# Graph layer 0 of a four-layer GNN kernel: sums of the second half's rows moved, block sums left to accumulating transfers

## The chip, the core and the metric

One core of a Trainium2 chip runs the whole program. The metric is the device time of one execution in microseconds (us), the median of several executions; lower is better.[...] PE is the matrix engine (TensorE), DVE the vector engine, ACT the scalar engine, POOL the GpSimd engine, SP the engine that issues most transfers.

## What is computed

```
# adj: 2708 x 2708, x: 2708 x 512
h = relu(layernorm(x));  d = (rowsum(adj) + 1) ** -0.5
x = x + relu(diag(d) (adj + I) diag(d) h @ W0)                  # layer 0
h = relu(layernorm(x));  x = x + norm(adj) h @ W1.T + b1          # layer 1
h = relu(layernorm(x));  x = x + relu(norm(adj + I) h @ W2)       # layer 2
h = relu(layernorm(x));  x = x + gated attention(h, adj)          # layer 3
```

Everything is float32. Only layer 0 is touched by the change.

## The kernel before

**Tiling.** The 2708 nodes are four quarters of 677. A quarter is five tiles of 128 rows and a tail; the tails of all quarters fill tiles 20 and 21. `h` holds the normalised features of all 22 tiles; "first half" means tiles 0 to 9 (quarters 0 and 1), "second half" tiles 10 to 21. The transposed adjacency lies in DRAM as blocks `yb[j, i, u]` of 128 x 1695 numbers (847.5 KB): quarter j of the sum, quarter i of the outputs, and u (0 or 1) one half of that quarter's 678 columns. 339 columns is the width of every large matmul.

**Two levels of fast matrix products.** `adj @ h` is done by seven outer products (a Strassen-Winograd form over halves) instead of eight: `OUTER` (line 376 after, the same table before) names for product p the feature operand (XA, XB, XC, XD are the two halves of `h` by the two halves of the features, overwritten as the work goes on) and the block operand: y11, y21, y22 as they lie in DRAM or the sums T1 = y12 + y11, T3 = y22 + y12, T2 = T3 + y11, T4 = T2 + y21, each with a multiple of the unit matrix. Every outer product is done for u = 0 and u = 1 by `multiply`, which is again seven products ("pieces") of five 128 x 339 matmuls: pieces 1, 6, 2, 7, 5, 4, 3 in program order. Before it, `inner_x` makes four small feature sums (128 x 640) and `inner_y` makes four block sums t1, t2, t3, t4 (128 x 1695 each) on DVE. Piece 6 reads t2, piece 7 reads t3, piece 5 reads t1, piece 4 reads t4. Behind the pieces DVE adds the results (`u2`, `u3`, `give`) out of PSUM into `agg`.

**Layer 0 has its own order**, `first_aggregate`. Row sums of `adj` must be known before `h` can be scaled, so the first half's degrees are summed on PE (`column_sums`: matmuls with a 32-column operand `first`) while the blocks arrive, then product 1 runs for u = 0, 1, then product 7 (u = 0, 1), and during product 7 the second half's degrees are summed (`other_degrees`): three blocks' worth per u out of T3's inner sums. Behind the second of these come twelve one-column matmuls that turn row sums into columns (line 346), roots on ACT and DVE (`rsqrt`, `rstd_of`), and the normalising activations of the second half (line 221, 128 x 512 each). Product 6 needs XA := -XD - XA (line 682), so it needs those. Then products 6, 2, 4 for u = 1 and again for u = 0, the tail rows (`tails`, quarters 0 and 1), product 5 (u = 0, 1), `tails` (2, 3), and the epilogue (line 754 and on).

**Block sums before.** T3 is made from two plain loads each (y22 and y12) and a DVE add (`third_sums`, line 644); T2 by DVE (line 651); both are also written to DRAM (`keep_o`, line 398) for later layers. T4 by DVE (line 723). T1 is made by a plain load of y12 and an accumulating transfer of y11 onto it (`first_sums`, line 697: `dma_start(..., accum_op=ALU.add)` on POOL's queue), then the unit matrix (line 410) is added by DVE.

**What sets the order.** A tile scheduler places each engine's instructions by readiness and program order; `tc.issue_after(i)` keeps the instructions in its scope behind instruction i in that placing. SP issues plain loads[...]; POOL issues stores and accumulating transfers. Waits come from buffers: `free` is a list of 847.5 KB buffers, and `more`, `early`, `spare` are buffers cut out of areas that layer 0 does not yet need (`ends`, `agg`, and the second half of `h`).

Of the kernel before, what the change touches and what calls it, by code (L numbers as in the profile page):

```python
# [8 lines left out]
FP = mybir.dt.float32  # L9
AF = mybir.ActivationFunctionType  # L10
ALU = mybir.AluOpType
# [26 lines left out]
def gnn_kernel(  # L38
# [172 lines left out]

    def shift_of(mv, scale, n):

        b = small_cols("sh", n)
        nc.vector.scalar_tensor_tensor(
            b[:, :n], mv[:, :n, 0], -1.0, scale[:, :n], ALU.mult, ALU.mult
        )
        return b

    def normalized(t, src, scale, shift):  # L220
        nc.scalar.activation(h[:, t, :], src, AF.Relu, bias=shift, scale=scale)

# [19 lines left out]
    def first_stats(ts):  # L242
        for t in ts:
            stats(h[:, t, :], mv0[:, t, :])


# [66 lines left out]

    def other_degrees(u, ys):

        if u == 0:
            parts[1, 1] = upool.tile([P, W], FP, tag="s", name="row")
        for b, blocks in ((0, (ys[1], ys[2])), (1, (ys[7],))):
            ps = ps_out.tile([P, W], FP, tag="out", name="dg_ps")
            tl = tail_place(b, u)  # L320
            column_sums(ps, [tl[:, 0], tl[:, 1]], blocks, parts[b, u])
        if u < U - 1:
            return
        columns = {}
        for b in range(2):
            columns.update(quarter_columns(2 + b, [parts[b, v] for v in range(U)]))
        columns.update((t, tail_columns(t)) for t in (NF, NF + 1))
        first_h(columns, NF - half)
# [10 lines left out]
    def first_h(columns, looped):  # L339
# [18 lines left out]
        nc.vector.tensor_mul(rstd[:, :n], rstd[:, :n], dinv[:, span])  # L358
        sh = shift_of(mv, rstd, n)
        for s, t in enumerate(ts):  # L360
            normalized(t, h[:, t, :], rstd[:, s : s + 1], sh[:, s : s + 1])

# [59 lines left out]


    at_u2, at_u3, at_end, at_t4 = [], [], [], []

# [16 lines left out]
    def inner_y(blks, u, loops, t3=None):  # L442
        o11, o12, o21, o22 = blks
        if loops:
            add_loops(o11, u, loops)
            add_loops(o22, u, loops)
        t1, t2, t4 = (tpool.tile([P, KT, W], FP, tag="t", name=f"t{k}") for k in (1, 2, 4))
        t3 = o12 if t3 is None else t3
        nc.vector.tensor_add(t1, o12, o11)  # L449
        nc.vector.tensor_add(t2, o22, t1)  # L450
        at_t4.append(nc.vector.tensor_add(t4, o21, t2).ins)  # L451
        nc.vector.tensor_add(t3, o22, o12)
        return {1: o11, 2: o21, 3: o22, 4: t4, 5: t1, 6: t2, 7: t3}
# [12 lines left out]

    def multiply(xs_, ys, u, dests):

# [14 lines left out]
        def give(a, b, ps, part, op):  # L483
# [5 lines left out]
            for fh, ih, how in dests:  # L489
# [3 lines left out]
                elif how == "added":  # L493
                    nc.vector.tensor_add(d, d, ps)
                elif how == "less":
                    nc.vector.tensor_sub(d, ps, d)
                else:
                    nc.scalar.copy(d, ps)
# [3 lines left out]
        v = upool.tile([P, W], FP, tag="v", name="v")  # L502
        nc.scalar.copy(v, pa)  # L503
        pb = bank("pb")
# [10 lines left out]
        product(pd, 5, True)  # L515
        give(1, 1, pd, u3, ALU.subtract)
        product(pc, 4, False)
        give(1, 0, pc, u2, ALU.add)
# [32 lines left out]
    def tails(self_loops, qs, loaded=None):  # L551

        for q in qs:
            blk, both = loaded[q] if loaded else tail_rows(self_loops, q)
            for u in range(U):
# [8 lines left out]
                for c in range(NC):  # L564
                    d = agg[:, c // 2, q // 2, c % 2, q % 2, u * W : (u + 1) * W]
                    nc.vector.tensor_add(d, d, ps[c])
            free.append(blk)
# [38 lines left out]
    def first_aggregate(epilogue):  # L606
# [9 lines left out]
        pieces = [(q, u) for q in range(2) for u in range(U)]  # L616
        places = spare + early
        for q, u in pieces:
# [11 lines left out]


        t3 = {0: [free.pop(0), free.pop(0), take(early), take(early)], 1: blks[0]}
        temps = spare + [take(early)]
        p1, p7 = (0, 0, "as it is"), (1, 1, "as it is")
        for u in range(U):
            for b in range(2):
                load_rows(*(tail_place(b, u)[:, s] for s in range(2)), yt[:, :, 2 + b, u])
        xs_ = inner_x(XA)
        multiply(xs_, ys, 0, [p1])
        ys = inner_y(blks[1], 1, 0, own_t3)  # L640

        def third_sums(u):
            for (a, b), blk, y in zip(QUAD, t3[u], temps):
                nc.vector.tensor_add(blk, blk, y)
                if a == b:
                    add_loops(blk, u, OUTER[7][2])
                keep_o(blk, "t3", a, b, u)

        def second_sums(u):
            for (a, b), t2, y in zip(QUAD, blks[u], t3[u]):  # L650
                nc.vector.tensor_add(t2, t2, y)
                keep_o(t2, "t2", a, b, u)

        for (a, b), blk, y in zip(QUAD, t3[0], temps):
            load_plain("y22", a, b, 0, blk)
            load_plain("y12", a, b, 0, y)
        with tc.issue_after(at_u2[-1]):
            third_sums(0)
        for (a, b), y in zip(QUAD, temps):
            load_plain("y12", a, b, 1, y)  # L660
        multiply(xs_, ys, 1, [p1])
        second_sums(0)
        by_halves(nc.vector.tensor_sub, XA, XA, XB)
        xs_ = inner_x(XA)
        ys = inner_y(t3[0], 0, 0, own_t3)
        last_sum = at_t4[-1]
        other_degrees(0, ys)
        for (a, b), blk in zip(QUAD, t3[1]):
            load_plain("y22", a, b, 1, blk)
        multiply(xs_, ys, 0, [p7])  # L670
        with tc.issue_after(last_sum):
            third_sums(1)
        first_x(range(half, NT))
        ys = inner_y(t3[1], 1, 0, own_t3)
        with tc.issue_after(at_u3[-1]):
            second_sums(1)
        with tc.issue_after(at_end[-1]):
            first_stats(range(half, NT))
        other_degrees(1, ys)
        multiply(xs_, ys, 1, [p7])  # L680
        first_part_of_both()
        by_halves(minus_sum, XA, XD, XA)
        free += t3[0][:2] + t3[1]

        def among(places):
# [4 lines left out]
            return free.pop(0)  # L690


        def first_sums(u, places):
            t1 = [among(places) for _ in QUAD]
            for (a, b), blk in zip(QUAD, t1):
                load_plain("y12", a, b, u, blk)
                nc.gpsimd.dma_start(blk, yb[a, b, u], accum_op=ALU.add)
            with tc.issue_after(at_u3[-1]):
                for (a, b), blk in zip(QUAD, t1):
                    if a == b:  # L700
                        add_loops(blk, u, OUTER[5][2])
                    keep_o(blk, "t1", a, b, u)
            return t1

        for u in reversed(range(U)):
            if u == 1:
                t2 = blks[1]
            else:
                t2 = [among(in_obuf) for _ in QUAD]
                for (a, b), blk in zip(QUAD, t2):  # L710
                    nc.sync.dma_start(blk, osum["t2", a, b, u])
            xs_ = inner_x(XA)
            multiply(xs_, inner_y(t2, u, 0, own_t3), u, [(0, 1, "added")])
            if u == 1:
                other_roots()
                nc.vector.tensor_sub(XB, XB, XD)
            y21 = [among(more) for _ in QUAD]
            for (a, b), blk in zip(QUAD, y21):
                load_plain("y21", a, b, u, blk)
            xs_ = inner_x(XC)  # L720
            multiply(xs_, inner_y(y21, u, 0, own_t3), u, [(0, 0, "added")])
            for (a, b), t4, y in zip(QUAD, t2, y21):
                nc.vector.tensor_add(t4, t4, y)
                keep_o(t4, "t4", a, b, u)
            free += y21
            if u == 0:
                rows = [tail_rows(True, q) for q in (0, 1)]
            xs_ = inner_x(XD)
            multiply(xs_, inner_y(t2, u, 0, own_t3), u, [(1, 0, "as it is")])
            if u == 0:  # L730
                t1 = first_sums(0, more)
            free += t2
        nc.vector.tensor_add(XC, XC, XA)
        tails(True, (0, 1), rows)
        ends_of_sums()
        xs_ = inner_x(XB)
        p5 = [(0, 1, "less"), (1, 1, "less")]
        multiply(xs_, inner_y(t1, 0, 0), 0, p5)
        free = [f for f in free if all(f is not e for e in more)]
        first = [f for f in t1 if all(f is not e for e in more)]  # L740
        t1 = first_sums(1, in_obuf)
        multiply(xs_, inner_y(t1, 1, 0), 1, p5)
        free += first + t1
        tails(True, (2, 3))
# [393 lines left out]
```

## Time and profile before

| what | us |
|---|---|
| median of 3 executions | 2141.94 (2141.34 to 2142.16) |
| the profiled execution, its own time | 2147.35 |
| its span from first to last instruction | 2145.6 |
| PE busy in the span | 2068.6 (96%) |
| DVE busy | 1438.6 (67%) |
| start of layer 0's epilogue on PE (line 754) | 374.04 |

Times inside the span are counted from its start. A busy PE here means a matmul in flight; a group of "x10" records of line 475 is one piece (five matmuls, each two records) and takes 2.86 us from the start of one piece to the next when nothing is in the way. In brackets at the end of a timeline row stands the idle time of that engine before the row and what ended it.

### The profile page before, as it was taken

The page shows a single profiled execution, that of the slowest core. Times are in us where ns is not written, and L with a number is a line of the kernel's source. Part 1 is how long each engine was busy: PE and PEld are TensorE (multiplying, and loading weights), DVE is VectorE, ACT ScalarE, POOL GpSimd, SP SyncE. Part 2 cuts the span into 40 slices and gives each one's busy share as a digit, 9 for nine tenths or more (in the row PEclk, how much of TensorE's full clock was granted, in tenths as well). Part 3 has the DMA queues.
Part 4 walks back from the last instruction along what each step waited for, and adds up shares of the span by engine and source line. Part 5 has one row for each costly group of instructions (what it writes and reads, how often), then busy time and mean ns, then how long its engine had stood idle before and what let it go on. Part 6 is the DMA issues. An engine that isn't in the chain of part 4 may idle for free.

```text
span 2145.6 us, 19944 instructions
## 1 busy us (share of the span) xinstructions
PE 2068.6 (96%) x7310; PEld 1289.0 (60%) x7310; DVE 1438.6 (67%) x2513; ACT 384.7 (18%) x755; POOL 173.7 (8%) x319
## 2 busy tenths in 40 slices
PE   5989979999999999999999999999999999999998
PEld 2555646556666645566664546666677666666664
DVE  3888847667666867777576879968537755666512
ACT  1111000222000010100001121000116534444401
POOL 0000010211000020200001130000001000000001
PEclk9999989999999999999999999999999999999999
DMA  9884695446454443644453656544541233233212
GB/s 351 346 336 154 191 281 189 161 153 211 164 177 167 148 165 137 234 164 156 162 183 123 218 196 211 176 156 156 192 166 72 96 101 103 91 101 100 80 41 64
DMA packets 78720, 358.05 MB, mean 167 GB/s; under 512 B 10540, under 2 KB 14508, under 8 KB 78624
## 3 DMA queue, kind: packets, MB, share of 16 engines
q1 hardware_dynamic: 51104, 250.98, 34.3%
q0 software_dynamic: 27520, 105.82, 14.6%
q8 instruction: 57, 0.93, 0.2%
q14 instruction: 39, 0.32, 0.0%
HBM read 294.61 MB, written 62.15 MB: 166 GB/s over the span
## 4 chain that ended last, share of the span: by engine, by line
PE 62%; issue 20%; DMA 8%; DVE 7%; POOL 2%; ACT 1%; SPq 0%; POOLq 0%; DVEq 0%; ACTq 0%
PE pa L475 13%; PE pc L475 12%; PE pd L475 12%; PE po L754 7%; PE pb L475 6%; PE pe L1045 4%; PE pt L526 3%; PE pg L893 3%; DMA obuf<-in_yb_dram 2%; DMA h<-in_x_dram 1%; PE pt L531 1%; DVE ends L846 1%; POOL ends L761 1%; DMA ends<-xs 1%; DMA osumt<-obuf 1%
## 5 line engine op out<-in xcount | busy, mean ns | idle before, releaser
L1045 PE MATMUL pe<-obuf,h 128*128 128x339 f32 x1280 | 372.9, 448 | 0.0
L475 PE MATMUL pa<-obuf,h 128*128 128x339 f32 x1050 | 324.0, 454 | 13.4 <-DVE h L420 8.5
L1045 PEld LDWEIGHTS pe<-obuf,h 128*128 128x128 f32 x1280 | 241.2, 189 | 126.4 <-issue 10.0
L754 PE MATMUL po<-ends,agg 128*128 128x512 f32 x640 | 281.4, 596 | 2.1 <-ACT ends L774 1.9
L475 PEld LDWEIGHTS pa<-obuf,h 128*128 128x128 f32 x1050 | 200.1, 192 | 121.4 <-issue 9.4
L754 PEld LDWEIGHTS po<-ends,agg 128*128 128x128 f32 x640 | 119.8, 190 | 144.8 <-issue 137.3
L475 PE MATMUL pd<-obuf,s 128*128 128x339 f32 x550 | 169.0, 454 | 13.3 <-DVE agg L492 13.3
L475 PE MATMUL pc<-t,h 128*128 128x339 f32 x560 | 173.8, 457 | 4.4 <-DVE u L513 4.4
L966 ACT ACTIVATE e<-r,nsr 128x339 f32<-128x339 f32 x352 | 170.7, 566 | 28.6 <-DVE obuf L970 11.7
L475 PE MATMUL pb<-t,s 128*128 128x339 f32 x560 | 169.3, 448 | 0.1
L475 PE MATMUL pd<-t,s 128*128 128x339 f32 x560 | 169.2, 448 | 0.0
L503 ACT COPY v<-pa 128x339 f32<-128x339 f32 x56 | 24.6, 440 | 758.4 <-PE pa L475 738.8
L475 PEld LDWEIGHTS pd<-obuf,s 128*128 128x128 f32 x550 | 105.6, 192 | 68.0 <-DVE agg L492 14.3
L475 PEld LDWEIGHTS pc<-t,h 128*128 128x128 f32 x560 | 108.1, 194 | 60.9 <-DVE u L513 6.0
L475 PEld LDWEIGHTS pd<-t,s 128*128 128x128 f32 x560 | 106.0, 189 | 54.2 <-issue 0.5
L475 PEld LDWEIGHTS pb<-t,s 128*128 128x128 f32 x560 | 105.7, 189 | 54.6 <-DVE s L420 0.7
L475 PE MATMUL pc<-obuf,s 128*128 128x339 f32 x450 | 136.1, 448 | 0.0
L475 PEld LDWEIGHTS pc<-obuf,s 128*128 128x128 f32 x450 | 85.3, 189 | 43.6 <-issue 0.5
L450 DVE TENSOR_TENSOR t<-obuf,t 128x1695 f32<-128x1695 f32 x55 | 105.4, 1917 | 0.0
L780 POOL DMA_DIRECT2D xs<-ends x66 | 35.9, 544 | 817.6 <-DVE ends L779 764.8
L451 DVE TENSOR_TENSOR t<-obuf,t 128x1695 f32<-128x1695 f32 x53 | 101.6, 1917 | 0.0
L449 DVE TENSOR_TENSOR t<-obuf 128x1695 f32<-128x1695 f32 x49 | 94.1, 1920 | 9.8 <-DMA obuf<-in_yb_dram 6.6
(247 smaller groups left out, 2184.2 us busy)
## 6 DMA issues: line engine op xcount, KB each, us to landing
obuf<-in_yb_dram SPq DMA_DIRECT2D x131, 847.5 KB, 4.6
obuf<-osumt SPq DMA_DIRECT2D x100, 847.5 KB, 4.5
osumt<-obuf POOLq DMA_DIRECT2D x23, 847.5 KB, 9.0
xs<-ends POOLq DMA_DIRECT2D x66, 256.0 KB, 2.3
ends<-xs POOLq DMA_DIRECT2D x66, 256.0 KB, 3.4
obuf<-in_yt_dram SPq DMA_DIRECT2D x32, 339.0 KB, 3.6
h<-in_yb_dram SPq DMA_DIRECT2D x11, 847.5 KB, 10.0
ends<-in_yb_dram SPq DMA_DIRECT2D x11, 847.5 KB, 6.2
```

Of the source, the lines that this page charges most:

```text
L449: nc.vector.tensor_add(t1, o12, o11)
L450: nc.vector.tensor_add(t2, o22, t1)
L451: at_t4.append(nc.vector.tensor_add(t4, o21, t2).ins)
L475: nc.tensor.matmul(ps, xs_[q][:, k, :], ys[q][:, k, :], start=start and k == 0, stop=k == KT - 1, skip_group_check=not start,)
L503: nc.scalar.copy(v, pa)
L526: nc.tensor.matmul(ps[c], h[:, NF, c * P : (c + 1) * P], tl[:, 0, :], start=start, stop=False)
L531: nc.tensor.matmul(ps[c], h[g, NF + 1, c * P : (c + 1) * P], tl[g, 1, :], start=False, stop=True)
L754: nc.tensor.matmul(po, cs[c], w_sb[:, c, :], start=(c == 0), stop=(c == NC - 1))
L780: nc.gpsimd.dma_start(xs[t], xt)
L893: nc.tensor.matmul(pk, cs[c], wg_sb[:, c, k, :], start=(c == 0), stop=(c == NC - 1))
L966: nc.scalar.activation(e[:, k], row, AF.Exp, bias=nsr[:, t, s : s + 1], scale=1.0)
L1045: nc.tensor.matmul(pe[c], h[:, t, c * P : (c + 1) * P], a, start=(t == 0), stop=False)
```

## The change

- The sums T3 of both u are made by a plain load of y22 and an accumulating transfer of y12 onto it (`accumulated`), issued from POOL. They no longer use `spare`, so the second half's x is loaded right behind the tail rows, ahead of product 1.
- The second half's mean and variance are made on ACT (`other_stats`: 12 activations with a summed output, twice) instead of DVE's `bn_stats`.
- `other_degrees(1, ...)` is called inside `multiply` of product 7, u = 0, behind piece 5, on the four T3 blocks themselves; `other_h` (the one-column matmuls, roots and normalising) inside `multiply` of product 7, u = 1, behind piece 1. The normalising activations are split in two halves of 256 features.
- T2 of u = 1 is summed behind the roots (line 722 after); T2 of u = 0 later, by loading the stored T3 and accumulating y11 onto it.
- T4 of u = 0 goes to the y21 buffers. T1 of u = 0 is T2 - y22 by DVE (`third_less`, line 775 after); T1 of u = 1 is y12 + y11 by accumulating transfers.
- agg[:, 0, 1] is copied from agg[:, 0, 0] by a transfer instead of ACT. `other_roots` and `XB - XD` (line 784 after) and `XC + XA` (line 794 after) move. Several `inner_y` are put behind an end of the product before them by `issue_after`.

```diff
+    def other_stats(ts, squares):
+        y = ytp.tile([P, 2, W], FP, tag="yt", name="y").rearrange("p s w -> p (s w)")[:, 0:D]
+        for t in ts:
+            if squares:
+                nc.scalar.activation(
+                    y, h[:, t, :], AF.Square,
+                    bias=mv0[:, t, 0:1], scale=-1.0, accum_out=mv0[:, t, 1:2],
+                )
+            else:
+                nc.scalar.activation(y, h[:, t, :], AF.Identity, accum_out=mv0[:, t, 0:1])
...
+        t3 = {0: early[:2]}
+        places = spare + early[2:]
...
+        def accumulated(blks, key, u, source):
+            for (a, b), blk in blks.items():
+                if key in PLAIN:
+                    load_plain(key, a, b, u, blk)
+                else:
+                    nc.sync.dma_start(blk, osum[key, a, b, u])
+                j, i = PLAIN[source]
+                last = nc.gpsimd.dma_start(blk, yb[j + a, i + b, u], accum_op=ALU.add)
+            return last.ins
+        def keep_all(blks, key, u, a_b=QUAD):
+            for a, b in a_b:
+                keep_o(blks[QUAD.index((a, b))], key, a, b, u)
...
-        def third_sums(u):
-            for (a, b), blk, y in zip(QUAD, t3[u], temps):
-                nc.vector.tensor_add(blk, blk, y)
-                if a == b:
-                    add_loops(blk, u, OUTER[7][2])
-                keep_o(blk, "t3", a, b, u)
...
+        came[0] = accumulated(dict(zip(QUAD, t3[0])), "y22", 0, "y12")
...
+        first_x(range(half, NT))
+        xs_ = inner_x(XA)
+        multiply(xs_, ys, 0, [p1])
+        ys = inner_y(blks[1], 1, 0, own_t3)
+        came[1] = accumulated(dict(zip(QUAD, t3[1])), "y22", 1, "y12")
+        multiply(xs_, ys, 1, [p1])
+        with tc.issue_after(at_v[-1]):
+            other_stats(range(half, NT), False)
+        by_halves(nc.vector.tensor_sub, XA, XA, XB)
+        xs_ = inner_x(XA)
+        with tc.issue_after(at_end[-2]):
+            ys = inner_y(t3[0], 0, OUTER[7][2], own_t3)
+        with tc.issue_after(came[1]):
+            keep_all(t3[0], "t3", 0)
+        other_degrees(0, ((ys[1], ys[2]), (ys[7],)))
+        y7 = {}
+
+        def second_piece():
+            with tc.issue_after(at_u3[-1]):
+                for k in (0, 3):
+                    add_loops(t3[1][k], 1, OUTER[7][2])
+            other_degrees(1, (t3[1][::2], t3[1][1::2]))
+            with tc.issue_after(at_end[-1]):
+                y7.update(inner_y(t3[1], 1, 0, own_t3))
+
+        multiply(xs_, ys, 0, [p7], (5, second_piece))
+        with tc.issue_after(at_v[-1]):
+            other_stats(range(half, NT), True)
...
+        multiply(xs_, y7, 1, [p7], (1, second_h))
+        with tc.issue_after(at_shift[-1]):
+            for t2, y in zip(blks[1], t3[1]):
+                nc.vector.tensor_add(t2, t2, y)
+        keep_all(blks[1], "t2", 1)
+        nc.sync.dma_start(agg[:, 0, 1], agg[:, 0, 0])
+        by_halves(minus_sum, XA, XD, XA)
...
+            with tc.issue_after(u3_of_6 if u == 1 else at_u2[-1]):
+                for k in (1, 0, 3, 2):
+                    nc.vector.tensor_add(t4[k], t2u[k], y21[k])
+            keep_all(t4, "t4", u)
+            def third_less(k, y, at):
+                a, b = QUAD[k]
+                if k > 0:
+                    load_plain("y22", a, b, u, y)
+                with tc.issue_after(at):
+                    nc.vector.tensor_sub(t2u[k], t2u[k], y)
...
+                third_less(0, y22[0], at_u3[-1])
+                third_less(2, y22[0], at_end[-1])
+                with tc.issue_after(at_end[-1]):
+                    nc.vector.tensor_sub(XB, XB, XD)
             xs_ = inner_x(XD)
+            multiply(xs_, inner_y(t4, u, 0, own_t3), u, [(1, 0, "as it is")])
...
+        third_less(1, y22[1], at_u2[-1])
+        third_less(3, y22[1], at_end[-2])
+        free += y22
+        with tc.issue_after(at_end[-1]):
+            rows = [tail_rows(True, q) for q in (0, 1)]
+            nc.vector.tensor_add(XC, XC, XA)
         tails(True, (0, 1), rows)
...
+        came = accumulated({QUAD[k]: t1[1][k] for k in (0, 1, 3, 2)}, "y12", 1, "y11")
         ends_of_sums()
         xs_ = inner_x(XB)
         p5 = [(0, 1, "less"), (1, 1, "less")]
+        for u in range(U):
+            more_loops = OUTER[5][2] - (OUTER[6][2] if u == 0 else 0)
...
+            with tc.issue_after(at_end[-3]):
+                ys = inner_y(t1[u], u, more_loops, own_t3 if u == 0 else None)
+            keep_all(t1[u], "t1", u, QUAD if u == 0 else QUAD[::3])
+            multiply(xs_, ys, u, p5)
```

## The prediction

> **What bounds the kernel now.** One core, PE clock 0.989 of full: nothing is throttled. The page gives PE 96% of the span, and its chain that ended last is PE for 62%, DMA 8%, DVE 7%. So over the whole program PE sets the time, and only PE's gaps and half-speed stretches can be won. The built program's queues differ from the old ones in layer 0 alone, so I asked for PE's waits between 57 us (product 1 begins) and 375 us (the epilogue begins):
>
> ```profile
> engine line waited for: us in total, times, longest us
> PE pd L475 <- DVE agg L492: 12.3, 1, 12.3
> PE pa L475 <- DVE h L420: 8.5, 1, 8.5
> ...
> PE pt L526 <- DVE agg L566: 2.0, 1, 2.0
> PE pd L346 <- DVE across L286: 1.8, 1, 1.8
> PE pc L475 <- DVE u L513: 1.6, 1, 1.6
> PE pd L346 <- DVE dt L160: 1.5, 1, 1.5
> ```
>
> Then PE's timeline around them (start, us, ..., idle before):
>
> ```profile
> 147.66 5.69 PE L475 MATMUL pc<-t,h 128*128 128x339 f32 x10
> 153.19 3.02 PE L475 MATMUL pd<-obuf,s 128*128 128x339 f32 x10
> 164.75 5.69 PE L475 MATMUL pa<-obuf,h 128*128 128x339 f32 x10 [8.53 <-DVE h L420]
> ...
> 282.49 3.02 PE L475 MATMUL pc<-t,h 128*128 128x339 f32 x10
> 297.77 5.74 PE L475 MATMUL pd<-obuf,s 128*128 128x339 f32 x10 [12.26 <-DVE agg L492]
> ```
>
> Two holes. From 141.5 to 172.8 product 7 ends and product 6 begins: one-column matmuls, roots, normalising and XA stand between. At 285.5 the last piece of product 4 waits for DVE, and DVE's own timeline says for what:
>
> ```profile
> 294.07 0.65 DVE L410 SCALAR_TENSOR_TENSOR obuf<-ident,obuf 128x128 f32<-128x128 f32 x3 [13.17 <-DMA obuf<-in_yb_dram]
> ```
>
> that is a T1 block whose accumulating transfer had not landed. Sum of what PE can win between 96.25 (end of product 1) and 374.04 (first epilogue matmul): the stretch is 277.8. Needed are 70 pieces at 2.857 (200.0), eight tail groups at 3.26 (26.1), degree sums 3.9 + 4.1, one-column matmuls 2.1: 236.2. **41.6 us are lost now.**
>
> **Two pages of the skill.** The Trainium skill, "TensorE: Matmul & The Clock Gate", section "Part 1: The HAM clock gate", says that the PE clock falls to half after an idle window of about 3.4 us and returns after as much busy time. The rows above agree in size: a piece behind 8.53 or 12.26 us idle takes 5.7 for 2.86, 2.83 lost each. But
>
> ```profile
> 316.43 2.35 PE L526 MATMUL pt<-obuf,h 128*128 128x339 f32 x4 [2.00 <-DVE agg L566]
> ```
>
> four records at 0.59 behind only 2.00 idle. I go by the trace: an idle of 2 us or more costs 2.83 besides.
> "DMA: Bandwidth & Descriptors", section "SWDGE vs HWDGE vs iDMA", says that only GpSimd's queue can accumulate, and that a transfer engine takes turns between that queue and the others. It states no price. The trace has one (last three columns: clock, DMA share, GB/s):
>
> ```profile
> 20.00:45.00 25.00, 20.82 (x161) 9.10 (x152) 11.84 (x40) 6.99 (x12) 0.00 (x0) 1.00 1.02 414
> ...
> 285.00:290.00 5.00, 0.51 (x2) 0.00 (x0) 0.00 (x0) 0.00 (x0) 0.00 (x0) 0.94 1.02 209
> ```
>
> With all engines full, plain loads run at 414 GB/s and accumulates at 209: a block of 0.868 MB takes 2.1 or 4.15 us. One at a time they are slower; from issue to landing line 697 shows
>
> ```profile
> DMA to landing us min/median/max: 7.5/10.8/17.3
> ```
>
> **The change, part by part.**
> *Start.* Four degree buffers for six: SP's fifth and sixth degree loads now wait for PE's sums at 19 to 22 us instead of going at 14.4. About five transfers (11 us) are then still in flight, so nothing starves; 0. Halved normalising readies XA sooner, but piece 2 at 57.31 (4.81) is slowed by the clock too; 0, at best -2.
> *T3 by transfers.* Takes eight sums (8 x 1.83 = 14.7) off DVE and swaps eight plain loads for eight accumulates. Work for the DMA from 50 us (the last degree block lands) to the last T3 block: 4 + 4 y22 and one y21 (9 x 2.1), tail rows 2.1, x 7.6, eight accumulates 33.2: 61.8, so it lands near 113. T3 of u = 0 lands by about 89; DVE wants it at 95. Of u = 1, DVE's unit adds come at 113 and PE's degree sums read the last block at 117. Slack 3 to 4 us: cost 0, and late by 6 if an accumulate costs 4.9, as the mixed stretch at 262 to 280 suggests. If late, DVE's `give` of piece 5 and t1 to t4 queue behind that unit add. SP's y21 and POOL's stores come behind in their queues; stores end near 128.
> *Statistics on ACT.* 24 x 0.73 (a 128 x 512 activation) = 17.5 on an engine 18% busy. First twelve: from x landing (74 to 86) to about 95, before the copy `v` at 101.8; second: 102 to 113, before the degree copies at 117. Hidden by PE's pieces; 0. DVE loses 9 us of bn_stats.
> *Product 7, u = 0.* `inner_y` is now put behind the last-but-one end of product 1 (94.0). In DVE's queue order XA, s, unit adds, t1, t3, t2 follow: t3 at 102.8, t2 at 104.7. PE's degree sums wait for unit adds and t3: **1.5 lost**. Piece 5 ends at 115.0.
> *Degrees behind piece 5.* 24 matmuls for 19: 4.3 for 4.1, to 119.3; pieces 4, 3 and u = 1's piece 1 cover the rest to 127.9. In that time DVE does t1, t3, t2, then t4 (its buffer is free at 122.3, behind piece 4), the ends and eight small copies: done at 127. The one-column matmuls follow without a wait, to 130.0; the old gaps of 1.8 and 1.5 go. Their 2 us of thin work may leave the clock low: 0 to 2.83, I take **1.4**.
> *Roots.* Deg to shift took 2.0 for the first half (54.4 to 56.4): shift at 132. ACT: twelve XD halves of about 0.37 (0.73 for 512, scaled) to 137, all 24 by 141. DVE: four T2 sums 7.3, XA's first half 141.9, second half behind piece 4 (144.5), t2 148.5, s2 149.7. PE ends u = 1 at 147.2, runs piece 1 to 150.0, then piece 6: no wait. The hole at 156 to 172 is gone.
> *Copy of agg by a transfer.* ACT loses 2.46; 1.39 MB from about 126, wanted at 158; 0.
> *Products 6, 2, 4, u = 1.* No wait by the same walk. u = 0: t2 of product 6 is 0.4 late. T2's loads and accumulates have from 140 to 205 at a DMA share near 0.5; 0. `other_roots` moves behind `u2`; 1 us of DVE, hidden.
> *Product 2, u = 0: a new wait.* DVE rows:
>
> ```profile
> 250.79 1.93 DVE L723 TENSOR_TENSOR obuf<-obuf 128x1695 f32<-128x1695 f32 x1
> 253.18 2.98 DVE L577 TENSOR_TENSOR agg<-agg 128x2712 f32<-128x2712 f32 x1
> ...
> 270.80 2.82 DVE L733 TENSOR_TENSOR h<-h 128x2560 f32<-128x2560 f32 x1
> ```
>
> Let T be its start on PE. The queue from `u2` (T + 6.0) holds four T4 sums, two `third_less`, XB - XD and then product 4's t1, t3, t2: nine 1695-wide sums at 1.83 (16.5), nine 339-wide at 0.42 (3.8), four feature sums at 0.73 (2.9), XB - XD 2.75: 26.0. So t2 is ready at T + 32.1; PE is at piece 6 at T + 25.7. Lost 6.4, less 0.5 of tail matmuls put into it, plus the clock: **8.7**. XB - XD is a cost of place: it stands ahead of t1.
> *End of product 4.* T1 of u = 0 comes from DVE in place of accumulates, so the 12.26 + 2.83 go. The tail rows are loaded before they are needed; the old 2.0 and its slow clock go.
> *Product 5: a second new wait.* Its `inner_y` stands behind the last tail adds, and `ends_of_sums` (2.9) ahead of it: after PE's last tail matmul DVE needs 0.5 + 0.2 + 2.9 + 0.6 + 3 x 1.83 = 9.7 to t2, PE has two pieces, 5.7. Lost 4.0 plus the clock: **6.8**. T1 of u = 1: its last buffer is a tail buffer, free near 290; load and accumulate take it to 303, wanted near 316; 0.
>
> **Sum.** 41.6 - 0.2 - (1.5 + 1.4 + 0.4 + 8.7 + 6.8 + 0.6 for small steps) = 22.0 won. The profiled execution took 2147.35 and would be 2125.3; against the median of 2141.94: **2120.0**.
>
> **Rivals.**
> *A. No new waits.* The two DVE-bound places are covered, because DVE catches up earlier than I walk; about 36 to 38 won: 2105. Against it: 26.0 us of work in a window of 19.7. Chance 0.17.
> *B. T3 is late by some us*, with the two queues in each other's way: 4.9 an accumulate and a late last y22 put PE's degree sums 6 off, plus the clock 2.83: 2129. Chance 0.18.
> *C. Accumulates run one by one.* If they hardly overlap, eight at 12.2 (the median near 280 to 300) from 52 end at 150; PE's degree sums, wanted at 117, wait 33 + 2.8, against 22 won: 2156, slower. It decides from 139, at 10.9 each. For it: the 10.8 median above. Against it: those waited in a full queue, which costs nothing twice. Chance 0.05; another 0.03 between B and C.
> *D. Nothing moves*, because the scheduler puts the late pieces back: its queue order on PE speaks against it. 0.02.
> My forecast 0.55: 2113 to 2126.
>
> **Range.** It runs from 2104 to 2134: below stands part of A, above C, D and a piece of B. 0.2% (4.3 us) is about what can be told from no change: faster 0.92, same 0.03, slower 0.05.
>
> **What would show it.** No PE wait above 2 us between 119 and 225 of the span; product 6's first piece near 147; waits of about 6 us ahead of product 4's piece 6 (u = 0, near 254) and 4 ahead of product 5's, both put down to DVE's t2; the epilogue's first matmul near 352. Wrong if PE's degree sums wait on DMA at 115, or if either of those two waits is missing.

## The result, and the profile after

The changed kernel takes 2150.75 us (median of 12 runs, 2146.91 to 2154.35), the kernel before beside it 2143.18 (12 runs, 2139.64 to 2148.96): ratio 1.0034, 95% interval 1.0024 to 1.0044. It is slower by 7.6 us; 2120 was forecast. Its profiled execution took 2146.91, with a span of 2144.9; it is the shortest of the twelve. One execution of e6 below, the one that was profiled, took 2527.43 us at a granted clock of 0.817; neither it nor its profile is used.

First PE's waits in layer 0 of the kernel after, as they were read for the kernel before (total, times, longest):

```profile
engine line waited for: us in total, times, longest us
PE pc L494 <- DVE u L534: 8.3, 1, 8.3
PE pb L494 <- DVE t L469: 3.6, 2, 3.3
PE pt L554 <- DMA obuf<-in_yt_dram: 2.2, 1, 2.2
PE pt L549 <- DVE agg L589: 2.1, 1, 2.1
PE pt L549 <- DMA obuf<-in_yt_dram: 1.9, 1, 1.9
```

The two old heads of this list, 12.3 at product 4 and 8.5 at product 6, are gone. A new one of 8.3, for `u`, stands in their place, one that the forecast did not have. PE's timeline of the kernel after at the places that the forecast named:

```profile
118.56 0.74 PE L292 MATMUL dg_ps<-obuf,first 128*32 128x339 f32 x5
119.22 3.12 PE L494 MATMUL pc<-t,h 128*128 128x339 f32 x10
...
130.27 0.36 PE L363 MATMUL pd<-ones,dt 128*128 128x1 f32 x2
130.50 4.79 PE L494 MATMUL pb<-t,s 128*128 128x339 f32 x10
...
149.40 3.02 PE L494 MATMUL pa<-obuf,h 128*128 128x339 f32 x10
152.26 3.02 PE L494 MATMUL pb<-t,s 128*128 128x339 f32 x10
...
261.73 1.50 PE L554 MATMUL pt<-obuf,h 32*128 32x339 f32 x2 [2.17 <-DMA obuf<-in_yt_dram]
263.54 5.18 PE L494 MATMUL pb<-t,s 128*128 128x339 f32 x10 [0.31 <-DVE t L469]
...
286.89 1.41 PE L549 MATMUL pt<-obuf,h 128*128 128x339 f32 x4 [2.06 <-DVE agg L589]
...
308.56 4.80 PE L494 MATMUL pb<-t,s 128*128 128x339 f32 x10 [3.32 <-DVE t L469]
...
327.41 5.66 PE L494 MATMUL pc<-t,h 128*128 128x339 f32 x10 [8.33 <-DVE u L534]
```

The hole between products 7 and 6 is closed: no bracket at 149.40 or 152.26, where 164.75 and 172.79 stood before. The degree sums end at 119.2 without a wait. Then come three places that cost: piece 6 of product 4 (263.54), the tail sums (286.89), and twice product 5 (308.56 and 327.41).

The needed time by stage is the one of the forecast (2.857 a piece, 3.26 a tail group and so on); what a stage took above it is lost. Stages go from the first piece of one product to the first piece of the next. The first and second profile of each kernel, in us (the second ones are the two unchanged repeats below):

| from PE's ... to ... | needed | lost before | forecast after | lost after |
|---|---|---|---|---|
| end of product 1, product 2 (u = 1) | 70.1 | 21.8, 19.4 | 3.1 | 4.3, 4.3 |
| product 2 (u = 1), product 4 (u = 0) | 80.0 | 0.0, 0.0 | 0.4 | 0.8, 0.8 |
| product 4 (u = 0), product 5 (u = 0) | 33.0 | 18.9, 15.7 | 8.7 | 15.2, 15.1 |
| product 5 (u = 0), product 5 (u = 1) | 20.0 | 0.1, 0.1 | 6.8 | 17.3, 17.7 |
| product 5 (u = 1), epilogue | 33.0 | 0.7, 0.7 | 0.6 | 1.4, 2.0 |
| sum | 236.1 | 41.5, 35.9 | 19.6 | 39.0, 39.9 |

So layer 0 wins 15 to 18 us at the roots, as was meant, and loses the same again, nearly all of it between the first pieces of product 5's two halves. VectorE's timeline of the kernel after in that stretch:

```profile
306.59 1.92 DVE L469 TENSOR_TENSOR t<-obuf,t 128x1695 f32<-128x1695 f32 x1
...
320.09 0.19 DVE L571 TENSOR_TENSOR obuf<-obuf,ident 128x32 f32<-128x32 f32 x1 [8.92 <-DMA obuf<-in_yt_dram]
322.03 0.17 DVE L571 TENSOR_TENSOR obuf<-obuf,again_ident 128x5 f32<-128x5 f32 x1 [1.74 <-DMA obuf<-in_yt_dram]
...
324.33 0.51 DVE L528 TENSOR_TENSOR u<-v,pb 128x339 f32<-128x339 f32 x1
326.29 0.65 DVE L430 SCALAR_TENSOR_TENSOR obuf<-ident,obuf 128x128 f32<-128x128 f32 x3 [1.44 <-DMA obuf<-in_yb_dram]
326.86 0.50 DVE L534 TENSOR_TENSOR u<-u,pc 128x339 f32<-128x339 f32 x1
```

VectorE is through with t2 (306.59) and soon after with t4, and it isn't busy when PE waits: it stands idle for 8.92 at a unit add of 0.19 on the tail rows that come after product 5, because they aren't loaded. VectorE takes its queue in order: behind that add stands `u2`, whose piece 6 was done at 313 and which starts at 324.33, and, past one more late load, that of product 3's first block, `u3` (326.86). PE starts its next piece 0.5 later.

### The profile page after: what moved, and what is told of

It reads as the page before. It is cut to its first block, busy times and chain, and to the rows that moved or that the text cites. A ratio compares the mean times of both kernels' runs of the same rounds, so it can differ in the third digit from the quotient of the medians.

```text
span 2144.9 us, 20028 instructions
## 1 busy us (share of the span) xinstructions
PE 2071.7 (97%) x7320; PEld 1289.3 (60%) x7320; DVE 1418.1 (66%) x2487; ACT 406.7 (19%) x826; POOL 180.9 (8%) x327
## 4 chain that ended last, share of the span: by engine, by line
PE 46%; issue 38%; DVE 7%; DMA 5%; POOL 3%; ACT 1%; POOLq 0%; SPq 0%; ACTq 0%; DVEq 0%
PE pa L494 10%; PE pc L494 10%; PE pd L494 9%; PE po L822 5%; PE pb L494 5%; DMA obuf<-in_yb_dram 3%; PE pg L961 3%; PE pt L549 2%; DMA ends<-xs 1%; POOL ends L829 1%; PE pt L554 1%; DVE ends L914 1%; POOL out_dram L1065 1%; POOL xs L848 1%; PE dg_ps L292 1%
## 5 line engine op out<-in xcount | busy, mean ns | idle before, releaser
L494 PE MATMUL pa<-obuf,h 128*128 128x339 f32 x1040 | 318.6, 451 | 8.1 <-ACT h L223 4.1
L494 PE MATMUL pb<-t,s 128*128 128x339 f32 x560 | 174.8, 459 | 3.6 <-DVE t L469 3.6
L1130 DVE COPY agg<-pe 128x339 f32<-128x339 f32 x16 | 7.5, 506 | 138.1 <-PE pe L554 138.1
```

The lines of the kernel that those rows point to most:

```text
L494: nc.tensor.matmul(ps, xs_[q][:, k, :], ys[q][:, k, :], start=start and k == 0, stop=k == KT - 1, skip_group_check=not start,)
```

## The experiments

**e1, e5: both kernels once more.** No edit. The first theory, called Q, was that VectorE's queue between products 2 and 5 takes the gain back; its rival, called R, that the later layers or other places lose.

> The changed kernel unaltered, for a second trace. Theory Q (the gain of 20 us at product 6 is real and DVE's queue between the end of product 2, u = 0, and product 5 gives it back): product 6's piece 6 again near 152 us of the span, layer 0's epilogue again near 370, and a time near 2151, the later layers like those of the kernel before to within 2 us. Rival R (layer 0 is no better than the trace shows because typical runs lose elsewhere): the epilogue near 370 and the later layers 5 us or more longer than in the kernel before.

> The kernel before, unchanged, for a second profiled execution and more timed runs. Theory Q (the changed kernel's loss lies in VectorE's queue between product 2 and product 5 alone): its typical epilogue start is the same as in its first profile, near 374, so the changed kernel is lucky in its own first profile and gains nothing there; time within 0.1% of before. Rival R (the changed kernel loses in other places than these too): this profile starts product 1 and the epilogue 3 to 5 us earlier than the first one of it did (epilogue near 370), which would leave the changed kernel 3 to 6 us behind already at the epilogue.

The changed kernel took 2148.64 (20 runs; ratio 1.0029, interval 1.0020 to 1.0037), the kernel before 2144.41 (12 runs, against 2143.73 of its other runs). The epilogue began at 373.27 after and at 371.25 before, in the first profiles at 370.16 and 374.04; the second one of before is nearer to R's 370 than to Q's 374, so the traces don't show that the changed layer 0 is ahead. From there to the end of the span the kernel after took 1774.7 and 1774.9, the kernel before 1771.6 and 1775.9: no loss in the later layers that is larger than this spread. But the first profile of before had lost 5.6 us in layer 0 that the second didn't; 1.7 of them are the wait for `agg` at 316.43 that the prediction showed (2.00), and 0.9 its four records at a low clock. PE's timeline of e5 has the same four at full clock:

```profile
315.25 1.41 PE L526 MATMUL pt<-obuf,h 128*128 128x339 f32 x4 [0.27 <-DVE agg L566]
```

Both profiled executions of the kernel before are also 4 to 5 us longer than its medians (2147.35 and 2149.01, the longest of its twelve). Where a typical execution of it saves that time, no trace shows.

**e2, e3: one suspect taken from VectorE's queue at a time.** The tail rows' loads and unit adds behind `u2` of product 5's second half:

```diff
-        tails(True, (2, 3))
+        with tc.issue_after(at_u2[-1]):
+            rows = {q: tail_rows(True, q) for q in (2, 3)}
+        tails(True, (2, 3), rows)
```

and, in the other kernel, the two sums of features that stand ahead of what PE waits for: `XB - XD` behind `u2` of product 4, `XC + XA` behind `u2` of product 5 (both u = 0):

```diff
-                with tc.issue_after(at_end[-1]):
-                    nc.vector.tensor_sub(XB, XB, XD)
...
+        with tc.issue_after(at_u2[-1]):
+            nc.vector.tensor_sub(XB, XB, XD)
...
-            nc.vector.tensor_add(XC, XC, XA)
...
+            if u == 0:
+                with tc.issue_after(at_u2[-1]):
+                    nc.vector.tensor_add(XC, XC, XA)
```

> The changed kernel, with the tail rows of quarters 2 and 3 loaded and completed behind u2 of product 5, u = 1, so that their four small DVE additions no longer stand ahead of u2 of product 5, u = 0. Theory Q: PE's wait of 8.3 us ahead of piece 4 of product 5, u = 0, and its slow clock (2.8) go, about -11: 2140, the epilogue near 359. Rival R: the time stays at 2149 to 2153.

> The changed kernel, with XB - XD put behind u2 of product 4, u = 0, and XC + XA behind u2 of product 5, u = 0, out of the way of product 4's t2 and of the tail sums (2.75 us of DVE each). Theory Q: piece 6 of product 4, u = 0, starts 2.8 earlier and the tails end 2 to 4 earlier, together -4 to -7: 2144 to 2147. Rival R: no change beyond 1.5 us. A third way: the wait for the tail rows in product 5 grows by what is won ahead of it, since it hangs on a transfer: no change in time, but the tails end earlier in the trace.

Theory Q missed in both: 2147.99 (ratio 1.0022, 1.0014 to 1.0030) and 2147.53 (1.0018, 1.0008 to 1.0028). In e3 the third way came, the one that was named beside Q and R. VectorE's timeline of e2 says why:

```profile
317.06 0.51 DVE L528 TENSOR_TENSOR u<-v,pb 128x339 f32<-128x339 f32 x1 [3.47 <-PE pb L494]
330.75 0.65 DVE L430 SCALAR_TENSOR_TENSOR obuf<-ident,obuf 128x128 f32<-128x128 f32 x3 [13.19 <-DMA obuf<-in_yb_dram]
331.32 0.50 DVE L534 TENSOR_TENSOR u<-u,pc 128x339 f32<-128x339 f32 x1
```

The tail rows are out of the way and `u2` goes at once; then VectorE stands 13.19 at the next late load, product 3's, which was hidden behind the first. In e3 the tails end 3 us earlier and the wait for `u` grows from 8.7 to 12.1, PE's rows of e1 and of e3:

```profile
329.87 5.64 PE L494 MATMUL pc<-t,h 128*128 128x339 f32 x10 [8.67 <-DVE u L534]
```

```profile
330.42 5.42 PE L494 MATMUL pc<-t,h 128*128 128x339 f32 x10 [12.14 <-DVE u L534]
```

PE comes earlier to loads that land when they did. So work taken off VectorE buys nothing here; the loads' time sets `u2` (e3) and `u3` (e2).

**e7, e8, e4: the column sums of product 5's first half earlier.** Between the two groups of tail sums instead of behind the last; alone (e7), with e2's edit (e8), with both others (e4).

```diff
-        tails(True, (0, 1), rows)
+        tails(True, (0,), rows)
+        y5 = inner_y(t2u, 0, OUTER[5][2] - OUTER[6][2], own_t3)
+        tails(True, (1,), rows)
...
-            with tc.issue_after(at_end[-3]):
-                ys = inner_y(t1[u], u, more_loops, own_t3 if u == 0 else None)
+            ys = y5
+            if u == 1:
+                with tc.issue_after(at_end[-3]):
+                    ys = inner_y(t1[u], u, more_loops, None)
```

> The changed kernel with one edit: the column-pair sums of product 5's first half are emitted between the tail rows' two groups, so that they stand ahead of the last tail sums on VectorE. The queue order puts two of the four unit adds of the last tail rows still ahead of u2, and product 3's unit adds behind u3. Theory Q: t2 is no longer late (3.6 goes), the wait for product 3's load goes, but u2 still waits for the tail rows' loads: 4 to 8 us of wait at product 5 stay, time 3 to 10 us below the changed kernel, near 2142. Rival R (the wait is one of transfers, whatever the order): the wait of 8 to 9 stays whole, time within 3 us of the changed kernel.

> Both edits: the sums of product 5's first half between the two groups of tail rows, and the loads and unit adds of the last tail rows behind u2 of product 5's second half. On VectorE nothing that waits for a transfer stands ahead of u2 and u3 of product 5 any more. Theory Q: no wait of product 5 for u above 2 us, time 12 to 15 us below the changed kernel, 2134 to 2138, as with the feature sums moved too (2133.75). Rival R (moving the feature sums XB - XD and XC + XA was what paid): 2142 or more.

> Both edits of the two kernels before this one, and product 5's inner_y for u = 0 put between the two tail quarters instead of behind the last tail sums. Theory Q: product 5, u = 0, has no wait left over 1 us: -11, -5 and -6 (3.3 of wait, 1.8 of slow clock, 1.2): 2127 to 2132, the epilogue near 350. Rival R: 2145 to 2151.

| kernel | us, median | ratio, 95% interval | lost, product 5 u = 0 to u = 1 | lost, from there to the epilogue |
|---|---|---|---|---|
| e7, sums early | 2136.91 | 0.9970, 0.9958 to 0.9983 | 1.1 | 7.9 |
| e8, and rows late | 2137.33 | 0.9962, 0.9945 to 0.9979 | 7.8 | 1.4 |
| e4, and feature sums late | 2133.75 | 0.9956, 0.9940 to 0.9973 | 0.4 | 6.1 |

The one edit of e7 wins 12 to 14 us, more than was expected of it: it brings not only t2 forward (no wait at product 5's piece 6, u = 0), it also brings the unit adds of that T1 block forward, and with them its store and the load of the tail rows, issued at 297 to 301 in place of 312.41. SyncE's timeline of e7:

```profile
297.20 0.87 SPq L563 DMA_DIRECT2D obuf<-in_yt_dram  x2
...
300.64 1.47 SPq L563 DMA_DIRECT2D obuf<-in_yt_dram  x2
```

That was not in the theory: Q spoke of the order alone. What e7 still loses lies in product 5's second half, where VectorE waits for T1's last accumulate (u = 1) and PE for t2 behind it. VectorE's timeline of e7, then PE's:

```profile
323.16 0.61 DVE L430 SCALAR_TENSOR_TENSOR obuf<-ident,obuf 128x45 f32<-128x45 f32 x3 [2.86 <-DMA obuf<-in_yb_dram]
```

```profile
327.91 6.02 PE L494 MATMUL pb<-t,s 128*128 128x339 f32 x10 [3.29 <-DVE t L469]
```

The prediction had this transfer at 303, wanted near 316, at no cost; in the changed kernel PE came too late to feel it. e8, which takes the rows out of the queue besides, shows the order at work once more: its time is that of e7, but its loss stands in the first half, with a wait of 4.94 that its theory Q excluded. VectorE's timeline of e8, then PE's:

```profile
313.19 0.51 DVE L534 TENSOR_TENSOR u<-u,pc 128x339 f32<-128x339 f32 x1 [1.93 <-PE pc L494]
322.69 0.65 DVE L430 SCALAR_TENSOR_TENSOR obuf<-ident,obuf 128x128 f32<-128x128 f32 x3 [8.99 <-DMA obuf<-in_yb_dram]
323.25 0.50 DVE L506 TENSOR_TENSOR s<-pd,u 128x339 f32<-128x339 f32 x1
```

```profile
323.81 5.62 PE L494 MATMUL pd<-obuf,s 128*128 128x339 f32 x10 [4.94 <-DVE s L506]
```

`u3` is through, and the same late load now holds up the sum behind it.

**e9: the chain itself.** The tail rows of quarter 2 are loaded into the buffer of T1's block (0, 0), u = 0; those of quarter 3 stand behind them in SyncE's queue. The last use of that block is its store for the later layers, which waits for the unit adds. Here it is stored right after its subtraction instead, without its unit adds; VectorE's order stays as in the changed kernel. By the code the later layers expect this block with one unit matrix in it (`OUTER`), and the block stored here still holds the two of T2: e9 shows what the chain costs and is no kernel to keep. Its expectation has this point wrong.

```diff
                 third_less(0, y22[0], at_u3[-1])
+                keep_all(t2u, "t1", u, QUAD[:1])
...
-            keep_all(t1[u], "t1", u, QUAD if u == 0 else QUAD[::3])
+            keep_all(t1[u], "t1", u, QUAD[1:] if u == 0 else QUAD[::3])
```

> The changed kernel with one store moved: block (0,0) of T1, u = 0, is stored for the later layers right after its subtraction and so without its unit adds (the later layers read that block without them); VectorE's order between product 4 and the epilogue is the same as in the changed kernel. The block is the buffer into which the next tail rows are loaded. Theory Q2 (the 8 to 9 us wait of product 5 is the last link of a chain: unit add, store on GpSimd's queue, load of the tail rows on SyncE's queue, unit add on VectorE, u2): the load goes 6 to 8 us earlier, near 306, the wait for u falls below 2 us, and the time is 6 to 11 us below the changed kernel, 2139 to 2144. Rival R2 (VectorE's own work, or the transfers' bandwidth, sets it): wait and time as in the changed kernel within 3 us, or the wait goes over whole to product 3's load behind it (8 us for pd <- s).

2140.12 (20 runs; ratio 0.9985, 0.9978 to 0.9992): 9 to 11 us won by the place of one store. GpSimd's and SyncE's timelines of the kernel after, then SyncE's of e9:

```profile
304.68 1.08 POOL L418 DMA_DIRECT2D osumt<-obuf  x2 [7.58 <-DMA obuf<-in_yb_dram]
```

```profile
312.41 3.19 SPq L563 DMA_DIRECT2D obuf<-in_yt_dram  x4
```

```profile
305.47 2.62 SPq L563 DMA_DIRECT2D obuf<-in_yt_dram  x4
```

In the kernel after, GpSimd's queue stands 7.58 at the store ahead, which waits for a T1 accumulate of u = 1; our store goes behind it, at about 305. It has to be read out before the load may overwrite the block: 312.4. The load lands at 320. In e9 the load goes at 305.47 and the wait for `u` is gone from PE's list; PE now waits 4.76 at a tail matmul for the same rows, since two of these were put ahead of piece 6 there. Theory Q2 stands: order decides who waits, but the chain store, load, unit add decides until when.

**e6, e10: the roots put back behind product 7.** In the changed kernel (e6) and in e7's (e10).

```diff
-        multiply(xs_, y7, 1, [p7], (1, second_h))
+        multiply(xs_, y7, 1, [p7])
+        second_h()
```

> Undoes one part of the change: the one-column matmuls, the roots and the normalising stand behind the whole of product 7's second half instead of behind its first piece. If the gain of that part was real and is given back elsewhere (theory Q), the hole between products 7 and 6 returns: PE waits near 8 to 12 us ahead of product 6, and the time is 12 to 20 us above the changed kernel. If the part was worth little, because what follows is bound by VectorE or by transfers anyway (rival R), the hole is there but the time is within 5 us of the changed kernel.

> The kernel with the early sums of product 5 (2136.91), with one-column matmuls, roots and normalising behind the whole of product 7's second half. Theory Q: with product 5 no longer bound by late transfers the roots' place shows whole, 18 to 22 us, 2155 to 2159, a hole of 8 to 12 us with its slow clock ahead of product 6. Rival R: 12 to 14 us, as it was in the changed kernel, 2149 to 2151, because VectorE catches up in the hole what it lacks at product 2 and 4.

e6 took 2160.5 to 2163.75 (three runs; ratio 1.0083, 1.0063 to 1.0103), 10 to 13 us more than the changed kernel, at or just below the 12 to 20 of its theory. e10 took 2152.43 (ratio 1.0041, 1.0031 to 1.0051), 15.5 more than e7, between the two expectations. PE's timeline of e10 has the old hole again, behind the one-column matmuls:

```profile
149.05 0.56 PE L363 MATMUL pd<-ones,dt 128*128 128x1 f32 x2
161.34 5.47 PE L494 MATMUL pa<-obuf,h 128*128 128x339 f32 x10 [11.73 <-DVE h L440]
```

From the end of product 1 to product 2 it needs 88.7, e7 74.4: 14.3. So the gain of this part was real. That 3 to 5 us of it (15.5 less 10 to 13) went into waiting for the loads of product 5 in the changed kernel is likely, but not shown, as e6 has no profile to read.

**e11, e12: two smaller places.** e7 with the degree sums behind all of product 7's first half; and e4 with the second of T1's four subtractions behind `u2` of product 4:

```diff
-        multiply(xs_, ys, 0, [p7], (5, second_piece))
+        multiply(xs_, ys, 0, [p7])
+        second_piece()
```

```diff
                 third_less(0, y22[0], at_u3[-1])
-                third_less(2, y22[0], at_end[-1])
...
+        third_less(2, y22[0], at_u2[-1])
         third_less(1, y22[1], at_u2[-1])
```

> The kernel with the early sums of product 5 (2136.91), with the second half's degree sums behind all of product 7's first half instead of behind its piece 5. The prediction's reading: pieces 4, 3 and the next piece 1 no longer cover the eight small copies, so PE waits 1 to 2 us for them ahead of the one-column matmuls, and VectorE's t1 to t4 come later: 2 to 6 us slower, 2139 to 2143. The other case: pieces 4 and 3 ahead of the degree sums give the last T3 transfer more time and nothing waits: within 2 us of 2136.91.

> The kernel with all edits so far (2133.75), and the second of the four T1 subtractions behind u2 of product 4's first half instead of ahead of its sums t1 to t4; on PE the first tail matmuls then stand behind product 4 and not between its pieces 1 and 6. Theory Q (VectorE's queue alone holds piece 6 at product 4): t2 is ready 3 to 4 us earlier, the 4.5 us of waits for tail rows ahead of piece 6 become one of 4 to 5 us for t2, 3 to 5 us won: 2129 to 2131. Rival R: the tail rows, whose buffer that subtraction frees, come later and PE waits for them behind product 4: 2133 to 2138.

e11: 2139.69 (ratio 0.9981, 0.9973 to 0.9990), 2.8 more than e7; in the trace 1.7 of it lie between product 1 and product 2. The place in the midst is worth that, by the prediction's reading. e12: 2132.41 (ratio 0.9945, 0.9931 to 0.9959), the fastest of all, but only 1.3 below e4, which six and five runs don't tell apart. PE's timeline of e12:

```profile
259.49 3.12 PE L494 MATMUL pb<-t,s 128*128 128x339 f32 x10 [1.01 <-DVE t L469]
...
275.88 2.52 PE L549 MATMUL pt<-obuf,h 128*128 128x339 f32 x8 [1.84 <-DMA obuf<-in_yt_dram]
...
284.88 4.89 PE L549 MATMUL pt<-obuf,h 128*128 128x339 f32 x8 [5.36 <-DVE obuf L571]
```

Piece 6 waits 1.01 in place of 4.5 for rows, and 5.36 come back behind the product, where VectorE stands 8.19 at a subtraction for its load: theory and rival are both half right.

## Why the prediction was wrong, point by point

- *The bound and the sum of 41.6*: right for the profile it was read from, but that execution had lost 5.6 more in layer 0 than the second one (35.9). The step "the old 2.0 and its slow clock go" counted part of this accident as a gain. Execution against execution, 2125.3 was forecast and 2146.91 came: 21.6 more, of which the table has 19.4 (39.0 for 19.6). The other 9 us to the medians come from taking the gain of one long execution over to the median of 2141.94: that execution ran 5.4 above it, the one of the kernel after 3.8 below its own.
- *Start, T3 by transfers, statistics on ScalarE*: costed at nothing, and no PE wait of the trace belongs to them. Product 1 begins at 55.99 and 58.02 after, 57.31 and 59.27 before. No wait for a transfer at 115.7. ScalarE takes 0.75 a tile for the sums and 0.85 for the squares (0.63 or 0.72, and a second instruction of 0.19 that reads the accumulator), 0.73 was assumed; it ends at 89.9 and 114.0, in time for both of its copies.
- *Degrees in the midst, roots behind piece 1*: right. The first piece of product 6 comes at 149.40 (147.2 was forecast, from a product 1 that began 1.3 later), piece 6 without a wait. The stage lost 4.3 against 3.1. The clock behind the one-column matmuls cost 1.8 (130.50: 4.79 for 3.02), taken at 1.4. The price of 2.83 behind any idle of 2 us or more was too high for the short ones: 1.6 behind 2.00 and 2.06 (316.43 before, 289.67 after, and in both cases eight tail matmuls of 1.51 for 0.85), 1.8 behind 3.32.
- *Product 2 and 4, u = 0*: right in mechanism and about in size: t2 came at T + 33.3 (32.1), 9.0 lost (8.7). That the tail matmuls put into this place would wait 1.88 and 2.17 for their rows was not seen; it cost nothing more, as t2 was later still (0.31).
- *"End of product 4: the tail rows are loaded before they are needed"*: wrong, 6.2 lost there for 0. `third_less` of the last block waited 2.68 for its load, `XC + XA` (2.82) stood ahead of the tail sums, and PE idled 0.80, 2.06 and 1.20 with a slow clock between.
- *"Product 5: a second new wait", 6.8*: **the step that failed.** The wait for t2 was there, 3.32 and a slow piece (4.80), as worked out. But the walk along VectorE's queue ended at t2. The next entries, unit adds on the tail rows (2, 3) and on product 3's first block, wait for loads that wait for a store; behind them stood `u2` and `u3`: 8.33 and another slow piece (5.66). The stage lost 17.3 to 17.7 for 6.8, the largest single miss; moving one store took 8 of it away (e9). The same question, "what is queued behind", was asked for T3 and not asked here; none of the rivals named it either.
- *Chances*: 0.05 for slower, all of it given to accumulates that run one by one; they don't: PE's degree sums wanted the last of the eight at 115.67 and didn't wait. The epilogue began at 370.16; 352 was the sign named.

What the medians say beyond the table stays open: they differ by 5 to 7.5 us, the sums of layer 0 by -2.5 to +4 between single profiles. The two profiles of each kernel aren't enough to place the last few us.

## What to carry to other kernels

Walk an in-order queue past the instruction you are after, to the next one that another engine needs; ask of each entry between when its load lands, and of each load what frees its buffer, a store in another engine's queue included. Where a transfer is late, moving work off the waiting engine only changes who waits (e2, e3, and e8 beside e7); move the start of the chain (e7, e9: 9 to 14 us by the place of a few sums or of one store). Before counting a wait as a gain to be had, look whether a second execution has it.

## What the hardware did that was not expected

PE need not be idle to lose its clock: 2.6 us of one-column matmuls without a gap (127.90 to 130.50) were followed by a piece of 4.79 for 3.02, at a granted clock of 0.63 from 130.50 to 135.10 and 1.00 in the 2.5 us before. The piece takes 4.79 in e1, e4, e7 and e8 too; in e10, where the one-column matmuls stand elsewhere, PE's timeline has it at full speed:

```profile
128.75 3.02 PE L494 MATMUL pb<-t,s 128*128 128x339 f32 x10
```

An idle of 2.06 was followed by matmuls at up to half speed (289.67: eight records in 3.50 us for 2.55; granted clock 0.65 from 288.20 to 293.10), and so was the one of 2.00 before (316.43; 0.55 from 316.40 to 320.10). The Trainium skill, "TensorE: Matmul & The Clock Gate", "Part 1: The HAM clock gate", speaks of an idle window of about 3.4 us; these rows show the drop behind less. Three stretches, 8.33, 11.73 and 4.94 idle, agree with it: the pieces behind take 5.66, 5.47 and 5.62.
